# Layer 1 of a graph network: the wait for a PSUM bank is moved from the first product of a half part to the last product of the half before it, and additions are issued by halves of two parts

## The chip, the cores and the metric

The kernel runs on one core of a Trainium2 chip, in one launch. The metric is the device time of one execution in microseconds. The engines in the profile are PE (matrix products; PEld is its weight load), DVE (vector), ACT (scalar), POOL (gathers) and SP (most other transfers).

## The reference

The reference is a relational graph network of two layers on 12500 nodes with 128 features and 200000 edges, sorted by destination. Cut to what matters:

```python
seg  = dst * 10 + edge_type              # edge_type: the largest of 10 attribute columns
xs   = x[src]                            # one row of 128 for each edge
sums = segment_sum(xs, seg)              # by destination node and relation
cnt  = segment_sum(ones, seg)
mean = (sums / max(cnt, 1)).reshape(N, 10, 128)
out  = einsum('nrd,rdo->no', mean, w_rel) + x @ root + bias
```

Layer 1 is this with a relu behind it, layer 2 the same on layer 1's result with its own weights. The input is added to the end, and a layer norm over the features follows.

## The kernel before, in words

The edges stand in NT = 1563 tiles of 128. Four tiles (QB) make a part, of which there are NPT = 391, and two tiles a half part. Layer 1 (`layer_1`) is one loop over parts p. What the loop issues in which order is each engine's program order; there is no other planner. An engine takes its instructions in that order, and each waits on semaphores for what it reads and for the buffer that it writes.

For each tile, these steps are issued:

- `hots` on DVE (L842): a 128 x 120 matrix that has, for each edge, the weight 1/count in the column of its destination (12 nodes) and relation (10). It is made one part ahead (AHEAD = 1).
- `gathered` on POOL (L835): an indirect transfer that brings a row for each of the 128 edges. The first 177 tiles (below NX, "plain") gather rows of the input alone. All later ones gather 256 wide from the table XH, which has a row of layer 1's input and a row of what layer 1 has already made for layer 2.
- `products` on PE (L1079): the gathered rows are the weights and the hot matrix the moving side, so that zp is features x (relation, node). Plain tiles have one product (l = 0), the others two (l = 0 and 1). A tile of two products takes 240 columns of a bank.
- `sum_into` on DVE (L868): zp is added to the sums `cc` at the place of the tile's nodes.

A half part shares one PSUM bank, and there are four such banks (`fixed`, zp0 to zp3) in turn. So the products of half h go to the bank that the additions of half h-4 have read. Each gather buffer of the later tiles holds the eight rows-of-128 slots of one part, and there are four of them (NEAR); the first gather of a part goes to the slot that the last tile of the part four earlier has used.

In step p, the order before is: fill the hot matrices of part p+1; gathers of part p; additions of the first half of part p-2 (BEHIND = 2); products of the first half of part p; other work that is due (`todo`, `jobs`); additions of the second half of part p-2 and, when a block of 256 nodes is complete, `finish`; products of the second half of part p; other due work.

`finish(k)` puts a block's ten relations through the weights (`projected`, L828 and L830, on PE), takes bias and relu (`a`, ACT, L747), and puts further work on `todo` at due times counted in tiles: the turned rows (`rows_out`, L953 on PE, two tiles later, kept by L960), and the products of the result with layer 2's weights (`projected_rows`, L936 on PE, into the one bank yb, a part apart each), which ACT copies out (L942) and SP stores (L944). The transposes at L297 and L998 are of the same kind; `cc` of a finished block is cleared by ACT (L797). Other lines of the profile: L816 and L820 move the ring of sums on, L623 and L625 count edges for later tiles.

The addition that a product's bank waits for is known to the framework, which puts the semaphore wait on the first product that writes the bank. That product also waits for its gather.

Of the kernel before, what the change touches and what calls it, by code (L numbers as in the profile page):

```python
# [13 lines left out]
ALU = mybir.AluOpType  # L14
# [10 lines left out]
WN = 12  # L25
KW = NREL * WN
WMAX = 120
GROUPS = ((4, 38.6), (2, 20.8))
G = 16
QB = 4  # L30
# [5 lines left out]
BEHIND = 2  # L36
# [34 lines left out]
def rgcn_resnorm_kernel(ctx: ExitStack, tc: tile.TileContext, x, src, dst, attr, w_rel1, root1, b1,  # L71
# [7 lines left out]
    nc = tc.nc  # L79
    N, C = x.shape  # L80
# [7 lines left out]
    NPT = len(parts)  # L88
# [35 lines left out]
    NX = T0 + RT  # L124
# [4 lines left out]
    def limit_of(t):  # L129

        return starts[max((k for k in seen_from if seen_from[k] <= t), default=K0) + 1] if t >= NX else starts[KGAP + 1]
# [30 lines left out]
    for l, (a, last) in enumerate(((0, SPLIT), (SPLIT, NR))):  # L162
        while a < last:
            b = a + 1
# [9 lines left out]
            a = b  # L174
# [67 lines left out]
    def next_of(kind, of):  # L242

        turn_of_[kind] += 1
        return of[(turn_of_[kind] - 1) % len(of)]
# [27 lines left out]
            nc.sync.dma_start(to[full:p, :m], bass.AP(a.tensor, a.offset + E - P - left, [[P, 1], [1, m]]))  # L273

    behind = mybir.DependencyInfo(mybir.DependencyClass.NoSync, mybir.DependencyReason.SCHED_ONLY)
    first_index = None

    def early(c, ins):
# [64 lines left out]
    bank = ps_c.tile([P, YB], F32, name="bank")  # L343
# [363 lines left out]
    def rows_in(k):  # L707

        if home[0] is prep:
            if k == NBLK - 1:  # L710
                xb = fin.tile([P, 1, C], F32, name="xbe")
            else:
                hbs[k] = prep.tile([P, 2, 2 * C], F32, name=f"hb{k % 2}")
                xb = hbs[k][:, :, :C]
        else:
            xb = home[0].tile([P, 3, C], F32, name="xb")
        rows_dma(xb, x, k, False)
        return xb

    def features_in(k, l, xb):  # L720

        n0, n, subs = block(k)
        last = "e" if k == len(ranges[-1]) - 1 else ""
        fT = fin.tile([P, (len(subs) if last else 3) * P], F32, name="fT" + last)
        if l:
            nc.sync.dma_start(fT[:, :n], hT[:, n0:n0 + n])
            return fT
        pt = ps_f.tile([P, YB], F32, name="pf")
        for t, h in subs:
            nc.tensor.transpose(pt[:, t * P:t * P + h], xb[:h, t, :], ident[:h, :h])  # L730
        nc.scalar.activation(fT[:, :n], pt[:, :n], AF.Copy)
        return fT
# [100 lines left out]
    def gathered(g, j, table, idx, n):  # L833

        nc.gpsimd.indirect_dma_start(out=g[:, j * C:(j + n) * C], out_offset=None, in_=table,  # L835
                                     in_offset=bass.IndirectOffsetOnAxis(ap=idx, axis=0))

    def hots(keys, weights, cols, n, m):

        oh = next_of("oh", hots_)  # L840
        for j in range(n):
            nc.vector.tensor_scalar(oh[:, j * m:(j + 1) * m], cols[:, :m], keys[:, j:j + 1], weights[:, j:j + 1],  # L842
                                    op0=ALU.is_equal, op1=ALU.mult)
        return oh

    def offsets(row, t0, n, limits, ring=True):

        lims = [limits(t0 + j) for j in range(n)]
        if ring:
            laps = [lap_of_tile(t0 + j) * RN for j in range(n)]  # L850
            lims = [(lo - a, hi - a) for (lo, hi), a in zip(lims, laps)]
            assert all(hi + WN <= RW for _, hi in lims)
        vals = nc.values_load_multi_w_load_instructions(  # L853
            row, engines=[DVE], min_val=min(a for a, _ in lims), max_val=max(b for _, b in lims),
            skip_runtime_bounds_check_because="clamped to these nodes on the chip")[1]
        return [nc.s_assert_within(v, a, b, skip_runtime_bounds_check_because="clamped to these nodes on the chip")
                for v, (a, b) in zip(vals, lims)]

    def sum_into(ls, zp, at, off, w):

        m = NREL * w
        if ls.stop - ls.start == 2:
            s = cc[:, :, :, ds(off, w)]
            z = zp[:, at:at + 2 * m].rearrange("c (l r n) -> c l r n", r=NREL, n=w)
        else:
            s = cc[:, ls.start, :, ds(off, w)]
            z = zp[:, at:at + m].rearrange("c (r n) -> c r n", n=w)
        nc.vector.tensor_tensor(s, s, z, op=ALU.add)  # L868

    class Later:  # L870

# [22 lines left out]
    ALL, ONE, TWO = slice(0, 2), slice(0, 1), slice(1, 2)  # L894
# [13 lines left out]
    def layer_1():  # L908

        todo = Later()  # L910
        done = 0
        zps, ohs, xbs, fTs = {}, {}, {}, {}
        offs, row = None, None

        def finish(k, t):

# [128 lines left out]
        for p in range(-AHEAD, NPT + BEHIND):  # L1045
            if p + AHEAD < NPT:
                t0, n = parts[p + AHEAD]
                ohs[p + AHEAD] = hots(keyE[:, t0:t0 + n], wE[:, t0:t0 + n], iotaP, n, KW)
            if p < 0:
                continue  # L1050
            t = p * QB
            if p < NPT:
                t0, n = parts[p]
                plain = t0 + n <= NX
                if not plain or p % 2 == 0:
                    g = next_of("g", gathers if plain else gathers[:NEAR])
                if not plain:
                    turn = used[id(g)] = 1 - used.get(id(g), 1)
                slot = [p % 2 * QB + j if plain else 2 * (QB - 1 - j if turn else j) for j in range(n)]
                for j in range(n):  # L1060
                    i = t0 + j
                    idx = idxE[:, i:i + 1]
                    if i < NX:
                        gathered(g, slot[j], x, idx, 1)
                    else:
                        gathered(g, slot[j], XH[:N + limit_of(i)], idx, 2)
                made = (g, ohs.pop(p), slot)
            if p == NPT - CP // 4:
                xbs[NBLK - 1] = rows_in(NBLK - 1)
                fTs[NBLK - 1] = features_in(NBLK - 1, 0, xbs[NBLK - 1])  # L1070
            def products(g, oh, slot, a, b):
                n = parts[p][1]
                for j in range(a, min(b, n)):
                    i = parts[p][0] + j
                    if j % 2 == 0:
                        zps[p, j // 2] = next_of("zp", fixed)
                    zp, o = zps[p, j // 2], j % 2 * 2 * KW
                    for l in (0, 1) if i >= NX else (0,):
                        nc.tensor.matmul(zp[:, o + l * KW:o + (l + 1) * KW], g[:, (slot[j] + l) * C:(slot[j] + l + 1) * C],  # L1079
                                         oh[:, j * KW:(j + 1) * KW], start=True, stop=True)  # L1080

            def sums(a, b, then=None):
                nonlocal done, offs, row
                q = p - BEHIND
                if q < 0:
                    return
                t0, n = parts[q]
                if not a and t0 % CT == 0:
                    row = rows_.tile([1, CT], I32, name="row")
                    nc.scalar.dma_start(row, b_r[t0 // CT:t0 // CT + 1, :])  # L1090
                if not a and t0 % G == 0:
                    m = min(G, NT - t0)
                    offs = offsets(row[:, t0 % CT:t0 % CT + m], t0, m, bounds)
                for j in range(a, min(b, n)):
                    i = t0 + j
                    if i and lap_of_tile(i) > lap_of_tile(i - 1):
                        ls = ALL if i >= NX else ONE
                        lap_begun(ls)
                        if lap_of_tile(i) * RN < lap:
                            todo.at(t + 3 * QB, lambda _, ls=ls: edge_cleared(ls))  # L1100
                    sum_into(ALL if i >= NX else ONE, zps[q, j // 2], j % 2 * 2 * KW, offs[i % G], WN)
                    if j % 2 or j == n - 1:
                        del zps[q, j // 2]
                if b < QB:
                    return
                if then:
                    then()
                while done < NBLK and t0 + n >= done_after(done):
                    finish(done, t)
                    done += 1  # L1110

            if p < NPT - 1:
                sums(0, 2)
                products(*made, 0, 2)
                todo.run(t - QB // 2)
                jobs.run(t)
                sums(2, QB)
                products(*made, 2, QB)
            else:
                jobs.run(t)  # L1120
                sums(0, 2)
                if p < NPT:
                    products(*made, 0, 2)
                sums(2, QB, p < NPT and (lambda: products(*made, 2, QB)))
            made = None
            todo.run(t)
        todo.run(END)
# [700 lines left out]
```

## Time and profile before

| | |
|---|---|
| runs | 3677.16, 3677.30, 3686.43 us; median 3677.3 |
| profiled execution | 3672.03 us, span 3670.2 |
| mean granted TensorE clock | 0.753 |
| layer 1 with gathers from XH | about 320 to 2395 us of the span |
| layer 2 | from about 2700 us |

Busy time is a share of the whole span and a mean over stages, so it is read by stage. A wait is named by what released it. "remote" is a release whose source the trace doesn't name, "issue" is time in which the engine waited for nothing that the profile shows. A row of the timeline gathers neighbouring instructions of one kind (x8 is eight of them), and the bracket at its end is the engine's idle time before it.

### The profile page before, as it was taken

The page shows a single profiled execution, that of the slowest core. Times are in us where ns is not written, and L with a number is a line of the kernel's source. Part 1 is how long each engine was busy: PE and PEld are TensorE (multiplying, and loading weights), DVE is VectorE, ACT ScalarE, POOL GpSimd, SP SyncE. Part 2 cuts the span into 40 slices and gives each one's busy share as a digit, 9 for nine tenths or more (in the row PEclk, how much of TensorE's full clock was granted, in tenths as well). Part 3 has the DMA queues.
Part 4 walks back from the last instruction along what each step waited for, and adds up shares of the span by engine and source line. Part 5 has one row for each costly group of instructions (what it writes and reads, how often), then busy time and mean ns, then how long its engine had stood idle before and what let it go on. Part 6 is the DMA issues. An engine that isn't in the chain of part 4 may idle for free. (4 is left out here: it accounts for less than half of the span.)

```text
span 3670.2 us, 37654 instructions
## 1 busy us (share of the span) xinstructions
PE 2319.0 (63%) x10645; PEld 1779.5 (48%) x10645; DVE 1991.3 (54%) x6410; ACT 511.8 (14%) x799; POOL 2287.4 (62%) x2430
## 2 busy tenths in 40 slices
PE   1557676767676767677666767653566666566444
PEld 0445565555555555565555655543534343333333
DVE  4646476767575757565655656358644232332332
ACT  1111111212121212121212121110000000000000
POOL 5663666666666666666666666556666666666665
PEclk7677787888887888878888878765667777677555
DMA  4553555455555555555555555542334443443222
GB/s 121 159 164 94 187 157 186 151 167 159 177 174 159 189 158 190 158 192 159 190 156 188 159 159 156 147 111 55 105 112 139 129 153 123 148 152 116 61 57 52
DMA packets 345316, 529.25 MB, mean 144 GB/s; under 512 B 55520, under 2 KB 225723, under 8 KB 345100
## 3 DMA queue, kind: packets, MB, share of 16 engines
q0 software_dynamic: 99552, 249.45, 23.9%
q1 hardware_dynamic: 218105, 264.48, 21.7%
q10 hardware_dynamic: 27443, 12.82, 1.2%
q8 instruction: 89, 1.46, 0.2%
q14 instruction: 127, 1.04, 0.1%
HBM read 372.75 MB, written 160.19 MB: 145 GB/s over the span
## 5 line engine op out<-in xcount | busy, mean ns | idle before, releaser
L835 POOL DMA_INDIRECT g<-XH,idxE x1386 | 1309.9, 945 | 769.7 <-issue 368.6
L1079 PEld LDWEIGHTS zp<-oh,g 128*128 128x128 f32 x5898 | 918.4, 234 | 396.5 <-DVE cc L868 180.1
L1079 PE MATMUL zp<-oh,g 128*128 128x120 f32 x5898 | 957.0, 320 | 228.6 <-DVE cc L868 132.3
L868 DVE TENSOR_TENSOR cc<-cc,zp 128x240 f32 (+1 forms) x1563 | 606.5, 388 | 816.1 <-remote 354.1
L835 POOL DMA_INDIRECT g<-YD,idxB x678 | 640.3, 944 | 342.4 <-issue 190.7
L936 PE MATMUL yb<-w,a 128*128 128x512 f32 (+1 forms) x576 | 354.9, 706 | 383.3 <-ACT ys L942 229.0
L842 DVE TENSOR_SCALAR oh<-bank,keyE,wE 128x120 f32<-128x120 f32 x1563 | 517.3, 393 | 0.0
L1620 PEld LDWEIGHTS zy<-oh,g 128*128 128x128 f32 x1168 | 244.8, 275 | 317.9 <-DVE cc L1650 119.1
L1620 PE MATMUL zy<-oh,g 128*128 128x12 f32 (+30 forms) x1168 | 258.4, 347 | 206.5 <-DVE cc L1650 114.6
L942 ACT ACTIVATE ys<-yb 128x512 f32<-128x512 f32 (+2 forms) x291 | 152.8, 525 | 1384.8 <-remote 612.0
L1533 PE MATMUL alone<-cc,w 128*128 128x512 f32 (+1 forms) x440 | 305.3, 782 | 31.6 <-issue 16.9
L936 PEld LDWEIGHTS yb<-w,a 128*128 128x128 f32 x576 | 111.0, 240 | 413.7 <-ACT ys L942 255.9
L828 PE MATMUL pf<-cc,w 128*128 128x256 f32 (+2 forms) x1040 | 254.9, 401 | 25.7 <-issue 13.4
L835 POOL DMA_INDIRECT g<-in_x_dram,idxE x177 | 167.3, 945 | 138.2 <-PE zp L1079 60.0
L828 PEld LDWEIGHTS pf<-cc,w 128*128 128x128 f32 x1040 | 208.4, 215 | 63.9 <-issue 26.0
L835 POOL DMA_INDIRECT g<-YD,idxE x177 | 168.2, 951 | 110.8 <-issue 62.7
L775 DVE TENSOR_TENSOR cc<-pf,x 128x256 f32<-128x256 f32 (+2 forms) x52 | 21.2, 409 | 358.9 <-remote 219.9
L797 ACT ACTIVATE cc<-zero 128x1280 f32<-128x1280 f32 x170 | 214.6, 1262 | 0.0
L1620 PEld LDWEIGHTS zq<-oh,g 128*128 128x128 f32 x542 | 110.8, 253 | 151.2 <-DMA g<-YD,idxB 74.0
L842 DVE TENSOR_SCALAR oh<-columns,keyB,wB 128x45 f32<-128x45 f32 (+35 forms) x678 | 176.8, 335 | 0.0
L1620 PE MATMUL zq<-oh,g 128*128 128x45 f32 (+33 forms) x542 | 122.9, 341 | 84.3 <-DMA g<-YD,idxB 59.5
L1650 DVE TENSOR_TENSOR cc<-cc,zy 128x12 f32 (+24 forms) x306 | 59.0, 193 | 142.6 <-remote 61.0
(265 smaller groups left out, 1528.4 us busy)
## 6 DMA issues: line engine op xcount, KB each, us to landing
cc<-SD SPq DMA_DIRECT2D x21, 2560.0 KB
SD<-cc SPq DMA_DIRECT2D x41, 1280.0 KB
YD<-ys SPq DMA_DIRECT2D x194, 256.0 KB
m<-in_edge_attr_dram SPq DMA_DIRECT2D x48, 672.0 KB
g<-XH,idxE POOLq DMA_INDIRECT x1386
YD<-ys SPq DMA_DIRECT2D x97, 128.0 KB
XH<-hb SPq DMA_DIRECT2D x44, 256.0 KB
g<-YD,idxB POOLq DMA_INDIRECT x678
```

The lines of the kernel that those rows point to most:

```text
L775: nc.vector.tensor_tensor(v[:p, s], pr[:p, s], xb[:p, s], op=ALU.add)
L797: nc.scalar.activation(cc[:, l, h * H:(h + 1) * H, o:o + n], zero[:, None, :n].to_broadcast([P, H, n]), AF.Copy)
L828: nc.tensor.matmul(po[:, :n], wsb[l][:, r, :], sums[:, r], start=(r == 0), stop=(w is None and r == NREL - 1))
L835: nc.gpsimd.indirect_dma_start(out=g[:, j * C:(j + n) * C], out_offset=None, in_=table, in_offset=bass.IndirectOffsetOnAxis(ap=idx, axis=0))
L842: nc.vector.tensor_scalar(oh[:, j * m:(j + 1) * m], cols[:, :m], keys[:, j:j + 1], weights[:, j:j + 1], op0=ALU.is_equal, op1=ALU.mult)
L868: nc.vector.tensor_tensor(s, s, z, op=ALU.add)
L936: nc.tensor.matmul(yb[:h, :m], fin_a[k][:, b * P:b * P + h], wsb[1][:, r:r + m // C, :], start=True, stop=True)
L942: nc.scalar.activation(ys[:h, :m], yb[:h, :m], AF.Copy)
L1079: nc.tensor.matmul(zp[:, o + l * KW:o + (l + 1) * KW], g[:, (slot[j] + l) * C:(slot[j] + l + 1) * C], oh[:, j * KW:(j + 1) * KW], start=Tr ...
L1533: nc.tensor.matmul(po[:, :n], wsb[1][:, r, :], sds[j][:, r, :n], start=(r == 0), stop=(r == NREL - 1))
L1620: nc.tensor.matmul(zp[:, o:o + w], g[:, at * C:(at + 1) * C], oh[:, j * w:(j + 1) * w], start=not second or j == 0, stop=not second or j = ...
L1650: nc.vector.tensor_tensor(s, s, zps[q][:, j * w:(j + 1) * w], op=ALU.add)
```

## The change

The additions are issued a half part earlier in program order. In step p the order is now: additions of the second half of part p-2, with `finish`; products of the first half of part p; other due work; additions of the first half of part p-1; products of the second half of part p; other due work. `sum_into` returns its instruction, and the last one issued is kept in `added`. The l = 1 product of a half's second tile then waits for it: `add_manual_dep` with a dependence of class Sync puts a semaphore wait on that product. In numbers, the additions of half h-3 stand ahead of the products of half h, and the last of these products waits for them. The next half's products go to the bank that those additions read, so that the first product of a half finds this wait already done. Plain tiles have no l = 1 product. At the end of the loop the two halves of a part's products go together. DVE's order among the additions is what it was; the fills of hot matrices, `finish` and other due work stand differently to them.

```diff
--- before.py
+++ after.py
@@ -273,6 +273,7 @@
             nc.sync.dma_start(to[full:p, :m], bass.AP(a.tensor, a.offset + E - P - left, [[P, 1], [1, m]]))
 
     behind = mybir.DependencyInfo(mybir.DependencyClass.NoSync, mybir.DependencyReason.SCHED_ONLY)
+    awaited = mybir.DependencyInfo(mybir.DependencyClass.Sync, mybir.DependencyReason.DATA)
     first_index = None
 
     def early(c, ins):
@@ -865,7 +866,7 @@
         else:
             s = cc[:, ls.start, :, ds(off, w)]
             z = zp[:, at:at + m].rearrange("c (r n) -> c r n", n=w)
-        nc.vector.tensor_tensor(s, s, z, op=ALU.add)
+        return nc.vector.tensor_tensor(s, s, z, op=ALU.add)
 
     class Later:
 
@@ -910,7 +911,7 @@
         todo = Later()
         done = 0
         zps, ohs, xbs, fTs = {}, {}, {}, {}
-        offs, row = None, None
+        offs, row, added = None, None, None
 
         def finish(k, t):
 
@@ -1076,13 +1077,14 @@
                         zps[p, j // 2] = next_of("zp", fixed)
                     zp, o = zps[p, j // 2], j % 2 * 2 * KW
                     for l in (0, 1) if i >= NX else (0,):
-                        nc.tensor.matmul(zp[:, o + l * KW:o + (l + 1) * KW], g[:, (slot[j] + l) * C:(slot[j] + l + 1) * C],
-                                         oh[:, j * KW:(j + 1) * KW], start=True, stop=True)
-
-            def sums(a, b, then=None):
-                nonlocal done, offs, row
-                q = p - BEHIND
-                if q < 0:
+                        ins = nc.tensor.matmul(zp[:, o + l * KW:o + (l + 1) * KW], g[:, (slot[j] + l) * C:(slot[j] + l + 1) * C],
+                                               oh[:, j * KW:(j + 1) * KW], start=True, stop=True)
+                        if l and j % 2:
+                            tc.add_manual_dep(ins.ins, added.ins.name, awaited, reason="the next products take that bank")
+
+            def sums(q, a, b, then=None):
+                nonlocal done, offs, row, added
+                if q < 0 or q >= NPT:
                     return
                 t0, n = parts[q]
                 if not a and t0 % CT == 0:
@@ -1098,7 +1100,7 @@
                         lap_begun(ls)
                         if lap_of_tile(i) * RN < lap:
                             todo.at(t + 3 * QB, lambda _, ls=ls: edge_cleared(ls))
-                    sum_into(ALL if i >= NX else ONE, zps[q, j // 2], j % 2 * 2 * KW, offs[i % G], WN)
+                    added = sum_into(ALL if i >= NX else ONE, zps[q, j // 2], j % 2 * 2 * KW, offs[i % G], WN)
                     if j % 2 or j == n - 1:
                         del zps[q, j // 2]
                 if b < QB:
@@ -1110,18 +1112,16 @@
                     done += 1
 
             if p < NPT - 1:
-                sums(0, 2)
+                sums(p - BEHIND, 2, QB)
                 products(*made, 0, 2)
                 todo.run(t - QB // 2)
                 jobs.run(t)
-                sums(2, QB)
+                sums(p - BEHIND + 1, 0, 2)
                 products(*made, 2, QB)
             else:
                 jobs.run(t)
-                sums(0, 2)
-                if p < NPT:
-                    products(*made, 0, 2)
-                sums(2, QB, p < NPT and (lambda: products(*made, 2, QB)))
+                sums(p - BEHIND, 2, QB, p < NPT and (lambda: products(*made, 0, QB)))
+                sums(p - BEHIND + 1, 0, 2)
             made = None
             todo.run(t)
         todo.run(END)
```

## The prediction

> **What bounds the kernel now.** I read the page's list of engines first, then the busy time by stage, the groups of lines in layer 1's steady stretch (320 to 2395 us), the waits there, and last the timeline. In the stage rows each pair is an engine's busy us and its instructions, with granted TensorE clock, DMA share and GB/s at the end.
>
> ```profile
> PE 2319.0 (63%) x10645; PEld 1779.5 (48%) x10645; DVE 1991.3 (54%) x6410; ACT 511.8 (14%) x799; POOL 2287.4 (62%) x2430
> core 0: us, PE busy (x) PEld busy (x) DVE busy (x) ACT busy (x) POOL busy (x), PEclk, DMA share, GB/s
> 62.00:320.00 258.00, 138.31 (x542) 104.55 (x543) 157.93 (x524) 41.27 (x70) 129.12 (x137) 0.67 0.44 134
> 320.00:2395.00 2075.00, 1450.81 (x7499) 1178.93 (x7499) 1284.94 (x3769) 408.11 (x570) 1304.26 (x1380) 0.82 0.54 167
> ```
>
> No engine is full: of 2075 us PE works 1451, POOL 1304, DVE 1285. So chains of waits set this stage. Its groups (count | busy us, mean ns | idle before it and what ended that):
>
> ```profile
> L835 POOL DMA_INDIRECT g<-XH,idxE x1380 | 1304.3, 945 | 765.4 <-issue 367.8 <-remote 194.0 <-PE zp L1079 161.8
> L1079 PE MATMUL zp<-oh,g 128*128 128x120 f32 x5533 | 878.9, 317 | 162.9 <-DVE cc L868 83.5 <-issue 60.9 <-DVE oh L842 5.9
> L868 DVE TENSOR_TENSOR cc<-cc,zp 128x240 f32 (+1 forms) x1386 | 556.8, 402 | 732.1 <-remote 308.9 <-PE zp L1079 226.7 <-issue 78.2
> L828 PE MATMUL pf<-cc,w 128*128 128x256 f32 (+2 forms) x935 | 225.2, 396 | 16.1 <-issue 13.4 <-DVE cc L868 1.1 <-PE zp L1079 0.6
> ```
>
> POOL's idle time splits in two. "issue" belongs to each gather: 1304.3 + 367.8 = 1672 us is what 1380 gathers cost back to back (1.21 each). The other 400 of the 2075 us POOL stands, and it stands for buffers that products have not yet freed. The waits (us, times, longest):
>
> ```profile
> POOL g L835 <- remote: 194.0, 91, 3.1
> POOL g L835 <- PE zp L1079: 161.8, 64, 7.9
> POOL g L835 <- PE pf L953: 8.3, 6, 1.4
> DVE cc L868 <- remote: 308.9, 101, 6.5
> DVE cc L868 <- PE zp L1079: 226.7, 65, 11.3
> PE zp L1079 <- DVE cc L868: 83.5, 60, 3.8
> PEld zp L1079 <- DVE cc L868: 122.0, 108, 4.0
> PEld zp L1079 <- issue: 147.6, 277, 4.7
> PE yb L936 <- ACT ys L942: 218.0, 68, 8.6
> PE pf L953 <- ACT a L747: 35.6, 22, 4.3
> PE pf L828 <- issue: 13.4, 25, 1.7
> ```
>
> One stop of POOL costs (194.0 + 161.8) / (91 + 64) = 2.3 us. The additions wait for products (308.9 + 226.7) far more than products wait for additions (83.5). Why products are late is seen only in the timeline (start us, duration, engine, line, count, idle before and its releaser):
>
> ```profile
> 1501.24 0.94 POOL L835 DMA_INDIRECT g<-XH,idxE  x1 [2.85 <-remote]
> 1501.70 1.22 PE L936 MATMUL yb<-w,a 128*128 128x256 f32 x2 [3.24 <-ACT ys L942]
> 1502.96 0.38 ACT L942 ACTIVATE ys<-yb 128x256 f32<-128x256 f32 x1 [1.31 <-PE yb L936]
> ...
> 1505.65 1.03 PE L936 MATMUL yb<-w,a 128*128 128x512 f32 x2
> 1506.74 1.05 PE L1079 MATMUL zp<-oh,g 128*128 128x120 f32 x8
> 1509.99 0.95 POOL L835 DMA_INDIRECT g<-XH,idxE  x1 [0.30 <-issue]
> 1512.84 0.84 DVE L868 TENSOR_TENSOR cc<-cc,zp 128x240 f32 x2 [3.47 <-remote]
> 1512.88 0.60 ACT L942 ACTIVATE ys<-yb 128x512 f32<-128x512 f32 x1 [8.38 <-remote]
> 1513.07 0.94 POOL L835 DMA_INDIRECT g<-XH,idxE  x1 [2.13 <-remote]
> 1514.96 0.47 PE L297 MATMUL pf<-ident,wp 128*128 128x128 f32 x1 [7.17 <-ACT fT L1005]
> ```
>
> PE has done L936 by 1506.68 and the products by 1507.79 and then idles for 7.17 us. Yet DVE, ACT and POOL, which wait for exactly these, all start at 1512.84 to 1513.07, about 2 us after POOL's last gather ended (1510.94). From 1501.24 to 1513.07 lie eight gathers at 1.25 us and such a stop: 11.8 us. While POOL stands, an answer comes at once:
>
> ```profile
> 300.38 1.03 PE L936 MATMUL yb<-w,a 128*128 128x512 f32 x2
> 301.44 0.60 ACT L942 ACTIVATE ys<-yb 128x512 f32<-128x512 f32 x1 [0.58 <-PE yb L936]
> ```
>
> Here POOL is in a stop of 36 us, and ACT follows 0.03 us after PE's end. The same holds right after a restart: L936 from 1501.70 to 1502.92 is answered at 1502.96, 1.72 us after POOL's first gather. So my reading, drawn from these places and not proved for all, is this: while POOL issues gathers back to back, PE's completions reach the others late, mostly all together at POOL's next stop; a short window after its restart is the exception. The stage's pace is then gathers per such cycle, and what counts is how many half parts PE can do on its own between two releases. Four banks give it four.
>
> **The change part by part.** The sum is made against the profiled execution, 3672.03 us (span 3670.2), which is 5.3 us under the median of the three runs (3677.3); I add 5.3 at the end. No matmul, addition, gather or transfer is added or removed, and SP's and POOL's queues keep their order. Number the half parts h (part p has 2p and 2p+1).
>
> (1) The wait for the bank. Before, the first product of half h+1 waits for addition h−3. Now that wait stands one product earlier, at the last product of h (the l=1 product of the odd tile), whose completion frees the gather buffer and lets addition h go. So PE can do three halves and three of the fourth's four products on its own, not four. Behind the waiting product stand on PE the rest of todo (L936, L953) and the next half. Where it binds: at most the 60 times that a product now waits for an addition. There the release brings halves h−3 to h−1; addition h−3 goes first (0.84 us a pair in the row at 1512.84), then the late product (0.32), so it ends about 1.2 us after the release, within the 1.72 us for which the window is shown open; then nothing is lost, since POOL still has buffers. If it misses the window, POOL makes one more stop: 2.3 us. Bounds: 60 × 2.3 = +138 us above, and below the gain that rival B works out, −57. I take 4 of 60, near the lower end, because 1.2 is under 1.72: **+9**.
>
> (2) The first product of a half loses its second wait. The weight loads' rows have 147.6 us of unexplained idle in 277 places, 0.53 each, which bounds it. PE idles over 600 of 2075 us in this stage and its queue is not what ends POOL's stops, so what covers it is POOL's own pace. Bounds −147.6 and 0; I take **0**, with the row at 1514.96, where PE idles 7.17 us for something else.
>
> The Trainium skill (Perfetto Trace Analysis, Identifying Dependency Chains) says that an instruction which waits on several engines may get separate semaphore instructions ahead of it. By that, the change saves one such instruction a half; were PE the bound, the sum would fall by up to those 147.6 us. The trace agrees that there are such gaps, not that they lie on the path.
>
> (3) The additions stand one half earlier in the program: addition h−3 now precedes products h. DVE's order among additions stays; only the four L842 fills and todo's DVE work stand one half later against them. DVE idles 732 us ahead of L868, for products: **0**. If that cover went, a fill of 4 × 0.39 us would stand ahead of an addition.
>
> (4) A finished block. Its L828 matmuls wait for addition 2p−3 and now come when PE has done half 2p−1, before products(p, 0–1), not after half 2p. So PE is two halves ahead there, where it was three. There are 935 / 20 = 47 of these; 25 wait now, for 13.4 us. Bounds: 0, and 47 stops more, 47 × 2.3 = +108. I take 2 of 47, near the lower row: **+5**.
>
> (5) L953 (the turned rows of a finished block) stays at its due time, so between it and L828 lie three halves of products, not two, and ACT's `a` (L747) has that much longer. PE's wait there is 35.6 us in 22 places; POOL's wait for it is 8.3. Bounds −35.6 and 0; I take POOL's own row: **−8**.
>
> (6) The first 177 tiles have no l=1 product and so no new wait; only (3) and (4) touch them: **0**. At the end, one part's products go together: some us at most, **0**.
>
> Sum: 3672.0 + 9 + 0 + 0 + 5 − 8 = 3678; with the 5.3 to the median **3683 us**, 0.2% above. About 0.3% (11 us) is what a measurement of this kernel can tell from no change, so this is "the same".
>
> **Rivals.**
>
> A, slower: three halves and three products instead of four. Where the late product misses the window, its completion comes only at the next stop; the half part is then missing from a cycle, POOL gets four gathers where it had eight, and one stop is added. It decides once release to completion takes longer than the window, shown open to 1.72 us and shut by 1506.7 (5.4 us after the restart at 1501.24): one L842 fill (1.6 us) ahead of the addition is enough. If half of the 60 places do, +69: 3683 − 9 + 69 = 3743; if all, about 3812. Against it: the 1.2 us above.
>
> The Trainium skill (Perfetto Trace Analysis, Matmuls) has a rule that points the same way: independent matmul groups should rotate through PSUM banks so that evacuation overlaps the next group's matmuls. This change gives up a quarter of the fourth bank's share of that; no run here shows yet what that is worth.
>
> B, faster: the places in which a product waits for an addition are what ends POOL's stops late. Then with the first product free to go on its gather alone, three products of a half are done before the release, and only one is left after it, where before all four of the next half stood behind the wait. Each of the 60 places gains up to three products, 3 × 0.32 us = 0.95, so −57 us; with L953's 35.6 gone too, −93. Half of both is 3677 − 46 = 3631. For it: POOL's waits end with a product in 64 cases. Against it: 91 end with "remote", a release of many at once.
>
> C, nothing: the wait moved one product is hidden wholly, as are (4) and (5): 3677.
>
> **How the numbers follow.** My forecast (with C, since both lie within 0.3%) 0.36; A and its kin in (4) 0.35; B 0.29. The range takes in half of A above, 3743, and B down to 3637, which leaves out about 0.1 at each end; the likeliest case alone is 3668 to 3692.
>
> **What would show it.** (1): the row "PE zp L1079 <- DVE cc L868" keeps its 60 places and POOL's stops (91 + 64) their number; under A both rise, by tens, and POOL's idle total of 765 us grows by the whole difference. (2): "PEld zp L1079 <- issue" falls well under 277 places and the time stays. (4): L828's idle of 16.1 us grows. (5): L953's 35.6 falls toward 0. Under B, POOL's 161.8 falls by tens. I am wrong if releases are not tied to POOL's stops, or if the time moves outside layer 1 (after 2395 us).

## The result: 0.35 to 0.40% slower

The changed kernel took 3693.6 us (median of seven), the kernel before 3677.3: a ratio of 1.0040, 95% interval 1.0028 to 1.0052. One of the seven runs of the changed kernel took 4694 us and is left out of the ratio. Timed again on another chip, where the kernel before takes 3638 us, it was 1.0035 (1.0019 to 1.0051). So the change costs 13 to 16 us. (Chips differ by 1%, so times are compared within one batch of runs, and between batches only the ratios to the kernel before in the same batch.)

The profile after ran in 3688.1 us, span 3686.4. First the steady stretch by stage and by groups, as shown of before. The line numbers are one higher than before: L836 is the L835 of before.

```profile
320.00:2395.00 2075.00, 1465.61 (x7461) 1184.97 (x7461) 1284.34 (x3765) 408.52 (x567) 1321.87 (x1381) 0.82 0.54 167
```

```profile
L836 POOL DMA_INDIRECT g<-XH,idxE x1381 | 1321.9, 957 | 754.0 <-issue 369.1 <-PE zp L1080 223.2 <-remote 133.7
L1080 PE MATMUL zp<-oh,g 128*128 128x120 f32 x5516 | 892.8, 315 | 313.7 <-DVE cc L869 224.9 <-issue 77.6 <-DVE moved L449 3.6
L829 PE MATMUL pf<-cc,w 128*128 128x256 f32 (+1 forms) x920 | 243.7, 431 | 8.6 <-DVE cc L869 5.5 <-DVE oh L843 1.2 <-PE yb L937 1.0
```

POOL's idle time *fell* (765.4 to 754.0 us), while its busy time rose by 17.6 us for one gather more: the mean gather went from 945 to 957 ns. That is not what I had looked for. (Four long gathers, shown below, are 12.7 us of the 17.6; the rest is the one gather more and some 3 ns on each of the others.) The waits of the same stretch:

```profile
POOL g L836 <- PE zp L1080: 223.2, 99, 9.1
POOL g L836 <- remote: 133.7, 60, 3.1
PE zp L1080 <- DVE cc L869: 224.9, 126, 7.7
PEld zp L1080 <- issue: 182.3, 378, 5.1
PE pf L954 <- ACT a L748: 7.9, 8, 1.9
```

Products wait for additions twice as often (60 to 126 places, 83.5 to 224.9 us), so the wait does move to where it is felt. But POOL's stops by products and "remote", 155 before, are 159, and cost 356.9 us against 355.8. In these two profiles, 141 us more of waiting on PE gave POOL no more to wait for.

What made gathers longer is seen in the timeline of after, at one of four places (near 1055, 1433, 1623 and 1814 us):

```profile
1054.72 3.94 POOL L836 DMA_INDIRECT g<-XH,idxE  x1 [0.30 <-issue]
1054.82 2.92 DVE L821 MEMSET cc<- 128x3440 f32 x1 [0.66 <-issue]
1057.66 0.18 DVE L562 CAST d_f<-d_i 128x169 f32<-128x169 int32 x1
1058.97 0.95 POOL L836 DMA_INDIRECT g<-XH,idxE  x1 [0.30 <-issue]
```

and of before, at the same clear of the ring's edge (L820 there):

```profile
1050.13 0.94 POOL L835 DMA_INDIRECT g<-XH,idxE  x1 [0.30 <-issue]
1050.31 2.92 DVE L820 MEMSET cc<- 128x3440 f32 x1 [0.67 <-issue]
1051.38 0.95 POOL L835 DMA_INDIRECT g<-XH,idxE  x1 [0.30 <-issue]
1052.63 0.95 POOL L835 DMA_INDIRECT g<-XH,idxE  x1 [0.30 <-issue]
1053.15 1.15 DVE L842 TENSOR_SCALAR oh<-bank,keyE,wE 128x120 f32<-128x120 f32 x4
```

The same clear lies beside the gathers in both. Before, three gathers pass it at 0.95 us each. After, one gather stands from the clear's start until 0.82 us after the copy L562 has ended: 3.94 us. What differs is the next instruction on DVE: a fill that reads its constants from PSUM (L842), or a copy from int32 to float, from SBUF to SBUF (L562). The clear is put on `todo`, and `finish` empties `todo` before it begins. With `finish` now ahead of `jobs.run(t)`, the clear stands right ahead of what `jobs` issues, and in four of eleven laps (turns of the ring) that is this copy. It has to be right ahead. In another lap of the changed kernel a small operation with inputs in SBUF (L433) stands between the two, and the gathers pass:

```profile
1245.37 2.92 DVE L821 MEMSET cc<- 128x3440 f32 x1 [0.66 <-issue]
1246.54 0.95 POOL L836 DMA_INDIRECT g<-XH,idxE  x1 [0.30 <-issue]
1247.79 0.95 POOL L836 DMA_INDIRECT g<-XH,idxE  x1 [0.31 <-issue]
1248.22 0.72 DVE L433 SCALAR_TENSOR_TENSOR limit<-tiles,limit 128x11 f32<-128x11 f32 x4
1248.86 0.24 DVE L562 CAST d_f<-d_i 128x169 f32<-128x169 int32 x1
```

The end of layer 1 is longer too. From the last gather of layer 1 to the first from YD, which is layer 2's table (so layer 2's first gathers lie well ahead of 2700 us), before and after:

```profile
2386.41 0.95 POOL L835 DMA_INDIRECT g<-XH,idxE  x1 [0.30 <-issue]
2390.29 0.29 PE L730 MATMUL pf<-ident,hb 84*128 84x84 f32 x1 [0.81 <-DMA hb<-in_x_dram]
2394.31 1.90 PE L1079 MATMUL zp<-oh,g 128*128 128x120 f32 x8
2397.14 0.94 POOL L835 DMA_INDIRECT g<-YD,idxE  x1 [9.79 <-PE zp L1079]
```

```profile
2393.40 0.95 POOL L836 DMA_INDIRECT g<-XH,idxE  x1 [0.30 <-issue]
2399.62 0.29 PE L731 MATMUL pf<-ident,hb 84*128 84x84 f32 x1 [1.84 <-DVE cc L869]
2403.99 3.68 PE L1080 MATMUL zp<-oh,g 128*128 128x120 f32 x16
2409.00 0.95 POOL L836 DMA_INDIRECT g<-YD,idxE  x1 [14.65 <-PE zp L1080]
```

With the block's work ahead of the first half's products, 16 records of products stand behind it and not 8, and POOL waits 14.65 us and not 9.79. This one repeats in every profile. With `finish` in the second half of the step this wait is 8.5 to 13.0 us in all nine profiles (before and the runs below); with the early `finish` it is 14.0 to 16.4 us in all five. The lowest and the highest, c0_before and e7_between:

```profile
2373.03 0.94 POOL L835 DMA_INDIRECT g<-YD,idxE  x1 [8.46 <-PE zp L1079]
2383.53 0.95 POOL L838 DMA_INDIRECT g<-YD,idxE  x1 [16.43 <-PE zp L1082]
```

By these timelines the 16.2 us between the two spans lie as follows: 2.3 before the first gather from XH (309.12 and 311.40 us), 4.7 from there to the last one, 4.9 up to the first from YD, and 4.3 behind it. The same two kernels in one later batch (c0_before, c1_after) have 2.5, 3.3, 6.8 and -11.1, so the last share changes from one execution to the next, and only the first three came out alike in both pairs.

### The profile page after: what moved, and what is told of

It reads as the page before. It is cut to its first block, busy times and chain, and to the rows that moved or that the text cites. A ratio compares the mean times of both kernels' runs of the same rounds, so it can differ in the third digit from the quotient of the medians.

```text
span 3686.4 us, 36935 instructions
## 1 busy us (share of the span) xinstructions
PE 2330.1 (63%) x10645; PEld 1782.6 (48%) x10645; DVE 1994.8 (54%) x6410; ACT 513.5 (14%) x799; POOL 2306.4 (63%) x2430
## 4 chain that ended last, share of the span: by engine, by line
PE 30%; issue 23%; DVE 20%; POOL 10%; another core or an unknown queue 10%; DMA 3%; DVEq 2%; ACT 1%; SPq 0%; ACTq 0%; POOLq 0%
PE zp L1080 13%; POOL g L836 10%; DVE oh L843 6%; PE pf L829 5%; DVE cc L869 5%; PE yb L937 5%; PE alone L1533 2%; DMA g<-YD,idxB 2%; DVEq L854 2%; PE zy L1620 1%; DVE cc L821 1%; DVE cc L1282 1%; DVE cc L1650 1%; ACT cc L817 1%
## 5 line engine op out<-in xcount | busy, mean ns | idle before, releaser
L836 POOL DMA_INDIRECT g<-XH,idxE x1386 | 1326.6, 957 | 759.0 <-issue 369.4
L1080 PE MATMUL zp<-oh,g 128*128 128x120 f32 x5898 | 972.9, 318 | 385.9 <-DVE cc L869 279.9
L1080 PEld LDWEIGHTS zp<-oh,g 128*128 128x128 f32 x5898 | 907.4, 229 | 572.2 <-DVE cc L869 323.6
L836 POOL DMA_INDIRECT g<-YD,idxB x678 | 642.5, 948 | 343.6 <-issue 187.4
L1533 PE MATMUL alone<-cc,w 128*128 128x512 f32 (+1 forms) x440 | 297.3, 762 | 12.7 <-issue 7.2
L829 PE MATMUL pf<-cc,w 128*128 128x256 f32 (+2 forms) x1040 | 272.2, 428 | 17.0 <-DVE cc L869 13.5
L829 PEld LDWEIGHTS pf<-cc,w 128*128 128x128 f32 x1040 | 228.4, 233 | 60.1 <-issue 12.9
L836 POOL DMA_INDIRECT g<-in_x_dram,idxE x177 | 167.6, 947 | 139.0 <-issue 43.5
L836 POOL DMA_INDIRECT g<-YD,idxE x177 | 168.1, 950 | 120.4 <-issue 62.2
```

The lines of the kernel that those rows point to most:

```text
L829: nc.tensor.matmul(po[:, :n], wsb[l][:, r, :], sums[:, r], start=(r == 0), stop=(w is None and r == NREL - 1))
L1080: ins = nc.tensor.matmul(zp[:, o + l * KW:o + (l + 1) * KW], g[:, (slot[j] + l) * C:(slot[j] + l + 1) * C], oh[:, j * KW:(j + 1) * KW], st ...
L1533: nc.tensor.matmul(po[:, :n], wsb[1][:, r, :], sds[j][:, r, :n], start=(r == 0), stop=(r == NREL - 1))
```

## The experiments

The change has three separable parts: the order of the additions, the place of `finish`, and the wait. Theory Q (my rival A): fewer products ahead cost the time. Theory F: the early `finish`. Theory N: neither. In the cuts of code, `...` stands for what is left out, and the comments are mine.

**e1_no_wait**: the change without the wait.

```diff
-                        if l and j % 2:
+                        if False:
```

> The changed kernel without its new wait: additions are issued one half part earlier and a finished block's work comes before the first half's products, but the wait for the bank stands at the first product of the next half, as before. Theory Q (the quarter: three products ahead in the last half part instead of four cost the time): back to the kernel before, 3675 to 3681 us, and products waiting for additions (83.5 us in 60 places before, 224.9 in 126 after) near the number of before. Theory F (the finished block's L828 matmuls, now issued with two halves ahead instead of three, cost the time): stays at 3690 to 3695 us. Theory N (neither; gathers of 4 us and the end of layer 1): 3688 to 3695 us with such gathers still there.

Measured: 1.0036 (1.0024 to 1.0048). Without the wait the loss stays, so Q isn't needed for it. Products wait for additions in 64 places (window 320 to 2360 us), near the number of before, and the four gathers of about 4 us are still there. Theories F and N both allow this.

**e2_first**: the wait at the first product of a half part.

```diff
-                        if l and j % 2:
+                        if i >= NX and not l and j % 2 == 0:
```

> The changed kernel with its wait moved further, to the first product of a half part: exactly three halves ahead, a whole half part less than before, not a quarter. Theory Q: four times the loss of the change, so some 60 us over the kernel before, 3725 to 3760 us, with POOL's stops in layer 1 up from about 160 to 200 or more. Theory F and theory N: as the changed kernel, 3688 to 3697 us.

Measured: 1.0047 (1.0030 to 1.0065), that is 17 us over before where Q asked for 60, and by the ratios 4 us over e1_no_wait, within the intervals. PE waits 299.0 us in 157 places (window 320 to 2360 us), yet POOL's stops by products and "remote" cost 332.6 us, no more than the changed kernel's 352.7 in that window. So the loss isn't in proportion to the lead that is given up, as Q has it.

**e3_finish_late**, and once more as **e9_wait_alone**: the wait, with `finish` in the second half of the step.

```diff
                 jobs.run(t)
+                if p >= BEHIND:
+                    finished(sum(parts[p - BEHIND]))     # the loop that calls finish, taken out of sums
                 sums(p - BEHIND + 1, 0, 2)
```

> The changed kernel with the finished block's work put back into the second half of the step, behind the first half's products; the new wait stays. Theory F: back to 3675 to 3681 us. Theory Q: no gain, 3688 to 3697 us, and the waits at L953 up again from 7.9 us toward the 35.6 of before. Theory N: as the changed kernel.

> The kernel of e3_finish_late once more, unaltered: the new wait, with the finished block's work in the second half, and so without the copy behind the clear. Theory P alone: 1.000 to 1.0015 (then the 1.0038 of before came from the batch). If the moved wait has a price of its own: 1.002 to 1.005, with no long gather.

Measured: 1.0038 (1.0023 to 1.0054) and 1.0030 (1.0014 to 1.0045), no long gather in either profile. So F alone is wrong too: the loss stays with the late `finish`, and the wait has a price of its own.

**e6_order**: the order of the additions alone, without wait and with the late `finish` (both edits above).

> The changed kernel without the new wait and with the finished block's work in the second half of the step: of the change only the place of the additions among DVE's fills and other due work is left, and the end of layer 1. Theory R, by the order of the additions alone: 1.003 to 1.005. If it is the sum of small terms (wait, block's work, end of the layer): 1.000 to 1.002. Theory L: 1.002 to 1.005, as n1_null.

Measured: 1.0003 (0.9988 to 1.0018). The order of the additions costs nothing that shows, and e6 against e9 and e3 is the wait alone: 0.27 and 0.35%, 10 to 13 us, uncertain by some 8 us in each. Where it goes the profiles don't show. Two rows of each, e6 first, same window (320 to 2360 us):

```profile
L836 POOL DMA_INDIRECT g<-XH,idxE x1374 | 1298.9, 945 | 741.8 <-issue 359.0 <-PE zp L1080 194.0 <-remote 150.9
PE zp L1080 <- DVE cc L869: 40.5, 40, 3.2
```

```profile
L836 POOL DMA_INDIRECT g<-XH,idxE x1374 | 1298.7, 945 | 741.2 <-issue 362.8 <-PE zp L1080 207.0 <-remote 160.6
PE zp L1080 <- DVE cc L869: 204.7, 98, 7.5
```

PE waits 164 us more and POOL's stops by these two releasers cost 23 us more, but its idle time as a whole and the gathers in the window are the same. The profiled executions are no help: e9's (3638.8 us) is the fastest of its runs, e6's (3647.4) one of the slowest. The price is measured, its place is open.

**c0_before**, **c1_after**, **n1_null**: the two kernels again, and the kernel before with `OB = 6` for 7.

> The kernel before, unaltered, timed as if it were a new one: a ratio of 1.000 whose interval holds 1. Its profile tells whether gathers of 4 us and the 3 ns longer gathers (949 ns against 946 in the changed kernel's profile) belong to the kernel (theory K: none here, 946) or to the single execution (theory X: they may show here too).

> The changed kernel, unaltered, once more: 1.003 to 1.005 of the kernel before. Theory K: its profile has four gathers near 4 us again, at the same gathers, and a median of 949 ns. Theory X: they may be gone with the time unchanged.

> The kernel before with six hot matrices instead of seven, which no engine waits for: the order of every queue is that of before. Theory R (what costs the time is the order of the additions, the block's work and the end of layer 1): 1.000, within 0.15%. Theory L (the kernel before is a lucky layout, and nearly any edit loses about 0.35%): 1.002 to 1.005.

Measured: 1.0004 (0.9989 to 1.0019), 1.0035 (1.0019 to 1.0051) and 1.0011 (0.9997 to 1.0025). An edit that changes no queue's order is not clearly slower, so the loss isn't what any edit would cost. c1_after has the four gathers near 4 us at the same laps, c0 and n1 have none, so they belong to the kernel (theory K). The 3 ns more of the other gathers do not: see the last section.

**e7_between**: one instruction between clear and copy, in the changed kernel.

```diff
         nc.vector.memset(cc[:, ls, :, RN:], 0.0)
+        nc.vector.tensor_scalar(spare, riotaP[:, :1], 1.0, 0.0, op0=ALU.mult, op1=ALU.add)   # both in PSUM
```

> The changed kernel with one instruction more: behind each of the 11 clears of the ring's edge (L821, 2.9 us) DVE multiplies one column that lies in PSUM by one, so that the int32-to-float copy of L562 no longer stands right behind the clear. Theory P (a copy from SBUF to SBUF that is next on DVE takes from POOL what it needs for a gather while the clear before it still runs): no gather over 1.5 us in layer 1, where the changed kernel has four with 12.7 us in excess, and 10 to 13 us less than the changed kernel, 1.000 to 1.001 of the kernel before. Rival W (the long gathers only stand where a stop would have stood; the wait itself costs the time): they may go, but the time stays at 1.003 to 1.005, with POOL's stops longer by as much.

```profile
1042.35 0.95 POOL L838 DMA_INDIRECT g<-XH,idxE  x1 [0.30 <-issue]
1042.45 2.92 DVE L822 MEMSET cc<- 128x3440 f32 x1 [0.67 <-issue]
1043.60 0.95 POOL L838 DMA_INDIRECT g<-XH,idxE  x1 [0.30 <-issue]
1045.30 0.15 DVE L823 TENSOR_SCALAR bank<-bank 128x1 f32<-128x1 f32 x1
1045.31 0.28 DVE L563 CAST d_f<-d_i 128x169 f32<-128x169 int32 x1
```

All long gathers are gone: one operation of 128x1 between clear and copy does it. The time is 1.0029 (1.0016 to 1.0042), 2 to 4 us under the changed kernel's 1.0035 and 1.0040, with intervals that overlap. Theory P holds for the gathers and not for the time, where it asked for 1.000 to 1.001. Rival W has the time right and its account wrong: it asked for longer stops, and POOL's stops by products and "remote" cost 343.6 us (window 320 to 2360 us), between the 333.9 of c1_after and the 352.7 of the first profile. The wait of 16.43 us at the end of layer 1 is still there.

**e8_cast**: the kernel before (with `OB = 6`) with such a copy behind each clear.

```diff
         nc.vector.memset(cc[:, ls, :, RN:], 0.0)
+        nc.vector.tensor_copy(spare, sparei)          # 128x168, int32 to float, SBUF to SBUF
```

> The kernel before (with six hot matrices, as n1_null) with an int32-to-float copy of 128x168, SBUF to SBUF, put right behind each of the 11 clears of the ring's edge. Theory P: 7 to 10 gathers of about 4 us in layer 1, each 3.1 us in excess, so 20 to 30 us more, of which stops of POOL may give some back: 1.004 to 1.008. Rival W (the copy isn't the cause): 11 copies of 0.2 us on an engine that idles, 1.000 to 1.001, no long gather.

```profile
1045.33 3.98 POOL L838 DMA_INDIRECT g<-XH,idxE  x1 [0.31 <-issue]
1045.47 2.92 DVE L822 MEMSET cc<- 128x3440 f32 x1 [0.66 <-DVE cc L871]
1048.32 0.18 DVE L823 CAST spare<-sparei 128x168 f32<-128x168 int32 x1
1049.61 0.95 POOL L838 DMA_INDIRECT g<-XH,idxE  x1 [0.30 <-issue]
```

Nine long gathers, made by eleven copies of 0.18 us. The profile page's row of all these gathers, in n1_null and here:

```profile
L835 POOL DMA_INDIRECT g<-XH,idxE x1386 | 1310.0, 945 | 745.0 <-issue 364.1
```

```profile
L838 POOL DMA_INDIRECT g<-XH,idxE x1386 | 1336.6, 964 | 736.2 <-issue 361.0
```

They are busy 26.6 us longer, POOL's idle time before them is 8.8 us shorter, and the time is 1.0059 (1.0037 to 1.0081), 0.48% or 17 us over n1_null, uncertain by some 9 us. So the long gathers are shown both ways, made here and taken away in e7_between. Their price is shown one way only: 17 us for nine is some 2 us for each, and by that estimate 8 us for the four of the change, where taking them away gave 2 to 4 us, within the noise.

The Trainium skill (SBUF — State Buffer, Who interferes with whom) says that a copy or cast on DVE can enter a two-port mode, in which DVE and GpSimd lock each other out of a shared port pair for a whole instruction, and that an instruction with at most one input in SBUF outside these modes, as a clear is, doesn't contend. The trace agrees that POOL's gathers stand beside such a copy (3.98 us for 0.95), though no row shows the copy's mode. It differs in when: the gather already stands during the 2.92 us of the clear ahead of the copy.

**e4_five** and **e10_five**: five banks for the products, in the order of before; the compared constants move from PSUM to SBUF. In e10 the fills are made by `scalar_tensor_tensor`.

```diff
-    bank = ps_c.tile([P, YB], F32, name="bank")
+    bank = keep.tile([P, YB], F32, name="bank")          # and OB = 6, ps_c gone
-        fixed = [... for i in range(4)]
+        fixed = [... for i in range(5)]
```

> The kernel before with five banks for the products instead of four; the constants that lay in the fifth (the row of numbers that the hot matrices are compared with) move to SBUF, and there are six hot matrices instead of seven to make room. Theory Q (what PE can do ahead on its own sets the pace): one half part more, so 40 to 60 us less, 3617 to 3640 us, with POOL's stops down from about 160 to 130. Its rival (something else ends POOL's stops; the banks have slack): 3670 to 3680 us. If the constants in SBUF slow or speed DVE, L842's mean of 393 ns moves and shows it.

> Five banks as in e4_five (the kernel before's order, the compared constants in SBUF), but the hot matrices of layer 1 are made by scalar_tensor_tensor with the weight spread over the row, an operation with two inputs from SBUF, in place of tensor_scalar, the same numbers. Theory P: the 49 long gathers (60 us in excess) of e4_five are gone for the most part, and POOL's stops stay at e4_five's 240 us against 296 to 320: 40 to 60 us less than the kernel before, 0.984 to 0.990. Rival (the fifth bank gives nothing, and the stops come back as the long gathers go): 0.998 to 1.003.

Measured: 1.0055 (1.0034 to 1.0076) and 1.0034 (1.0016 to 1.0052). e4 misses every theory; e10 lies just above its rival's 0.998 to 1.003. In e4, the gathers in the window 320 to 2360 us, and one place:

```profile
L834 POOL DMA_INDIRECT g<-XH,idxE x1370 | 1371.1, 1001 | 670.0 <-issue 366.2 <-remote 148.8 <-PE zp L1078 122.2
907.28 1.55 DVE L613 TENSOR_TENSOR eqb<-bank,kh 128x1344 bf16<-128x1344 f32 x1
907.49 2.16 POOL L834 DMA_INDIRECT g<-XH,idxE  x1 [0.30 <-issue]
```

POOL's stops did fall (271.0 us by these two releasers; 344.9 in e6_order, same window, four banks), and the gathers took as much more: nine long ones beside a clear, where the fill behind it now reads SBUF alone, and 49 of 1.1 to 2.3 us beside L613, whose inputs now both lie in SBUF; n1_null has none above 1.1 us. In e10, whose fill reads two inputs from SBUF, both numbers are the same. What a fifth bank alone is worth stays open; a version that beats the kernel before was not found.

## Why the prediction was right or wrong, by its steps

The time lies in the range. The likeliest value, 3683 us, was 10 us too low, and 3693.6 lies just above the likeliest case (3668 to 3692), toward rival A and its kin in (4), which I had given 0.35. But A's mechanism, more stops of POOL, is not what the first profile shows. So part of the agreement is luck, as the steps show.

- (1) The wait, +9: the size was right (e6 to e9 and e3: 10 to 13 us, with (2) in it), by luck, since the working was not. I sized it as stops of POOL. Their number hardly rose with the change (155 to 159); from e6 to e9 it rose from 160 to 175, with 23 us more, but POOL's idle time as a whole did not. And e2_first, which gives up a whole half part of lead, doesn't cost four times as much. So rival A's price for each place does not hold, nor does my reading that the stage's pace is set by how many half parts PE can do on its own, at least between three and four of them.
- (2) The second wait, 0: not measured by itself, since it goes with (1) in every run. The program did lose instructions (37654 before, 36935 after; 37597 in e1_no_wait, where the wait stays at the first product), most of them semaphore instructions of the weight loads (1032 before, 353 after). Yet the row that I named as a bound, "PEld zp <- issue", rose from 277 to 378 places where I had it fall. Whatever those gaps are, taking these waits away did not lessen them.
- (3) Order of additions, 0: right by e6_order, 1.0003 (0.9988 to 1.0018).
- (4) The block's work, +5 by L828's wait: here the step failed. The 25 places and 13.4 us that I took for waits are idle time for which the profile names no wait ("issue"); the wait for additions was 1.1 us. With the change that became 5.5 us, and L828's idle time fell, 16.1 to 8.6 us. The early `finish` alone costs 0.36% (e1_no_wait), some 13 us. One part of it is this: `finish` empties `todo`, the clear L821 moves with it and comes to stand ahead of the copy L562, and four gathers take 4 us. I had counted what `finish` issues on PE and not what it flushes on DVE, and I had put todo's DVE work at nothing for an idle DVE, without asking whom it stops. By e8_cast's price, an estimate, the four are some 8 us; another part is in (6).
- (5) L953, −8: its wait fell as forecast (35.6 to 7.9 us) and gave nothing that can be seen: e1_no_wait, which has the same place of `finish`, isn't faster.
- (6) The end of layer 1, 0: under-sized. POOL's wait there grew by 4.9 us, as much as the +5 of step (4), and it goes with the early `finish` (14.0 to 16.4 us against 8.5 to 13.0). I had named time that moves behind 2395 us as a sign of being wrong. This is such time, and some third of the change.

The parts don't add: the wait alone 0.30 to 0.38%, the early `finish` alone 0.36%, both 0.35 to 0.40%. That POOL's idle time gives back part of a long gather is seen in e8_cast, whose gathers are 26.6 us longer and whose idle time is 8.8 us shorter; that the wait and the long gathers share the same slack in this way is argued, not shown. The reading that PE's completions come late while POOL issues gathers was not tested by any run.

## What to carry to other kernels

When a block of work is moved, list what it flushes and issues on every engine, and look at what then stands next to what: an engine with much idle time can still hold up another. Make a two-by-two of the parts (each alone, both, none) before believing one of them; here each alone cost about as much as both. If one gather in hundreds is four times as long, look at what DVE runs beside it, and at what is next on DVE.

## What was not expected of the hardware

A 2.92 us clear on DVE, which gathers otherwise pass at 0.95 us, holds a gather to its end and some 0.9 us beyond if the next DVE instruction is a copy from int32 to float, from SBUF to SBUF, of 128x169 (128x168 in e8_cast). One tiny instruction on PSUM between them lifts this (e7_between), and it can be made at will (e8_cast, nine of ten full clears). Being in SBUF isn't enough: L433 (128x11) and L484 (128x6) behind the clear hold nothing. Which of form, size and place decides was not tested.

Gathers have two lengths from one execution to the next, for the whole run: medians of 946 and 949 ns for those from XH. The changed kernel had both. Its gathers of layer 2, with their means, in the first profile and then in c1_after:

```profile
L836 POOL DMA_INDIRECT g<-YD,idxB x678 | 642.5, 948 | 343.6 <-issue 187.4
```

```profile
L836 POOL DMA_INDIRECT g<-YD,idxB x678 | 641.1, 946 | 335.2 <-issue 185.2
```

Over 2241 gathers 3 ns are 7 us, about half of what is measured here, so one profile against one other can't carry an explanation of this size. What sets the length is not known.
